# A cross-attention and FFN kernel: transposes and scores of one pair in turn, and the end of attention in parts of one pair

## The chip, the cores and the metric

The kernel runs on one core of a Trainium2 chip. A core has five engines with a queue each: TensorE (PE; its weight loads are shown apart as PEld), VectorE (DVE), ScalarE (ACT), GpSimd (POOL) and SyncE (SP), which mostly issues DMAs. They run side by side and wait for each other on semaphores. TensorE writes to PSUM, which has 8 banks; DVE and ACT empty them. The metric is the device time of one execution in microseconds (us); lower is better.

## The reference

32 batches of 100 rows of 256 features attend to a context of 361 rows each, with 16 heads of 64; after that comes an FFN of 1024 features with quantised weights and activations. All data are float32.

```python
x = x + _L0_xattn_ref(_layernorm(x, axis=-1), ctx_1024, ctx_1024, WQ, WK, WV, WO, mask)
x = x + _L0_ffn_ref(_layernorm(x, axis=-1), W1, b1, W2, b2)

# attention
Qh = jnp.einsum('btd,hdk->bhtk', Q, WQ)
Kh = jnp.einsum('btd,hdk->bhtk', K, WK)
Vh = jnp.einsum('btd,hdv->bhtv', V, WV)
logits = jnp.einsum('bhtk,bhsk->bhts', Qh, Kh) / jnp.sqrt(dk)
logits = logits + mask * -1000000000.0
attn = jax.nn.softmax(logits, axis=-1)
Ah = jnp.einsum('bhts,bhsv->bhtv', attn, Vh)
A = jnp.transpose(Ah, (0, 2, 1, 3)).reshape(Ah.shape[0], Ah.shape[2], -1)
return A @ WO

# FFN: both linear layers on integers, the scale from the whole tensor's minimum and maximum
h = _qlinear(x, W1, b1)
h = jax.nn.gelu(h, approximate=False)
out = _qlinear(h, W2, b2)
```

The scale of the activations is taken over all rows of all batches, so the FFN cannot begin before the attention of the last batch is complete.

## The kernel before

The attention is a list of steps. A step is one batch and some of its 8 pairs of heads: batch 0 is cut into steps of 2, 2 and 4 pairs, batch 31 into 4, 2 and 2, and each of the 30 batches between is one step of all 8 pairs ("whole-batch steps"). TensorE's order is exactly the order in which the program issues its instructions; the other engines' orders are set by a scheduler, which keeps the order of dependent instructions and the extra orders that the program states with `follow(a, b)` (a after b on one engine, without a semaphore).

In step i TensorE runs, in this order:

1. `weights_T(i - 1, pair)` for each pair of the step before (L405, tile pt). The softmax weights p of a head are transposed in three chunks, the lower and the upper half of the rows side by side in two 64-row tiles of the array, each into a bank of its own. One bank is copied to SBUF (tile pT) by DVE (L416), the other by ACT (L418).
2. `scores(i)` (L364, tile sc): two heads of a pair side by side, again in two 64-row tiles, one bank each. DVE adds the mask, writes p and finds the row's minimum m of the negated scores in one instruction (L376); this frees the bank. ACT takes the exponential in place and sums the row (L379). Then DVE takes reciprocals of four heads' sums at a time (L387) and multiplies each head by its own (L391).
3. `attend(i - 1)` (L434, tile av): values times transposed weights, four pairs to a bank, copied to aT by ACT (L441).
4. `v_part` (L276, tile pv): the values of this batch, six banks, copied by DVE (L283).
5. Work on groups of four batches: layer norm and its transposes (ptx L325), queries (pq L337), output projection (py L470) and its transposes back (po L484); for the last group the projection by batch, `project` (po L454).
6. `k_part` (L245, tile pk): the keys of the next step, one bank a pair, copied to kT by ACT (L252).

All these tiles take PSUM banks from one pool of 8, in the order in which they are issued. So a new tile waits until the tile that stands eight before it has been emptied.

`residual(b, y)` adds the projection to x, keeps minimum, maximum and moments, and for all batches but the last leaves `normalize(b)` (L132, on DVE) for later, for it needs a power that GpSimd computes. For the last batch the root is taken on ACT (L504, then the table of Gelu at L507). The main loop runs the waiting `normalize` calls in the next step, after a value copy.

After the loop comes the tail of the last step (batch 31, pairs 6 and 7): `project(B - 1, range(4))`, the transposes of both pairs, projection chunk 4, `attend` for both pairs, and chunks 5 to 7. ACT loads the table with the square root (L385, tile g0) at the end of `scores` of the last step. Then the maximum over all rows sets the quantisation, and the FFN starts.

Of the kernel before, what the change touches and what calls it, by code (L numbers as in the profile page):

```python
# [8 lines left out]
F32 = mybir.dt.float32  # L9
BF16 = mybir.dt.bfloat16  # L10
I16 = mybir.dt.int16
AF = mybir.ActivationFunctionType
ALU = mybir.AluOpType
# [8 lines left out]
BIG = 3.4e38  # L22
# [5 lines left out]
def kernel(  # L28
# [15 lines left out]
    nc = tc.nc  # L44
    P = 128
    B, T, D = x.shape
# [48 lines left out]
    def follow(a, b):  # L95

        tc.add_manual_dep(a.ins, b.ins.name, ORDER)
# [31 lines left out]
    def normalize(b, after):  # L129

        xb = xg[b // G][:, b % G, :]
        i = nc.vector.tensor_scalar(  # L132
            xb, xb, mv2[:, b, 0:1], rstd2[:, b : b + 1], ALU.subtract, ALU.mult
        )
        follow(i, after)
# [13 lines left out]
    with ExitStack() as att:  # L149
# [30 lines left out]
        def bank(name):  # L180
            return psum.tile([P, 512], F32, tag="ps", name=name)
# [165 lines left out]
                    -1.0 / DK**0.5, None, ALU.mult,  # L347
                )

        def scores(i):  # L350


            b, first, n = steps[i]
            g, j = b // G, b % G
            heads = range(2 * first, 2 * (first + n))
            rsum = small.tile([TP, 2 * NHP], F32, tag="rsum", name=f"rsum{i}")
            r = small.tile([TP, 2 * NHP], F32, tag="r", name=f"r{i}")
            for h0 in heads[::4]:
                four = range(h0, h0 + 4)
                pss = {}  # L360
                for h in four:
                    pair, k = divmod(h, 2)
                    pss[h] = bank(f"sc{i}_{h}")
                    nc.tensor.matmul(  # L364
                        pss[h][:TP, :S],
                        qbuf[pair // PAIRS][
                            k * DK : (k + 1) * DK, pair % PAIRS, j, :, :
                        ].rearrange("p k t -> p (k t)")[:, :TP],
                        kT[k * DK : (k + 1) * DK, pair, :],
                        start=True,  # L370
                        stop=True,
                    )
                for h in four:
                    s = pb[:, h, :S]
                    m = small.tile([TP, 1], F32, tag="m", name=f"m{i}_{h}", bufs=8)
                    found = nc.vector.tensor_tensor_reduce(  # L376
                        s, pss[h][:TP, :S], maskt, 1.0, BIG, ALU.add, ALU.min, m
                    )
                    nc.scalar.activation(  # L379
                        s, s, AF.Exp, bias=m, scale=-1.0, accum_out=rsum[:, h : h + 1]  # L380
                    )
            if i == len(steps) - 1:

                g0 = small.tile([T, 1], F32, tag="g0", name="g0")
                nc.scalar.activation(g0, rsum[:T, heads[-1] : heads[-1] + 1], AF.Sqrt)  # L385
            for h0 in heads[::4]:
                last = nc.vector.reciprocal(r[:, h0 : h0 + 4], rsum[:, h0 : h0 + 4])  # L387
                follow(last, found)
                for h in range(h0, h0 + 4):
                    s = pb[:, h, :S]  # L390
                    nc.vector.tensor_scalar(s, s, r[:, h : h + 1], None, ALU.mult)  # L391
            return last

        pTs, aTs = {}, {}

        def weights_T(i, pair):


            h0 = 2 * pair
            pts = [bank(f"pt{i}_{pair}_{k}") for k in range(2)]  # L400
            for h in range(2):
                for c in range(NSC):
                    for k in range(2):
                        ks = slice(k * RH, k * RH + TH)
                        nc.tensor.transpose(  # L405
                            pts[k][:SC, (h * NSC + c) * TH : (h * NSC + c + 1) * TH],
                            pb[ks, h0 + h, c * SC : (c + 1) * SC],
                            ident[ks, ks],
                        )
            pT = pTs[i, pair] = p1.tile(  # L410
                [SC, 2 * NSC, 2, TH], F32, tag=f"pT{pair}", name=f"pT{i}_{pair}"
            )
            for k in range(2):
                src = pts[k][:SC, : 2 * NSC * TH].rearrange("p (c t) -> p c t", t=TH)
                if k == 0:
                    nc.vector.tensor_copy(pT[:, :, k, :], src)  # L416
                else:
                    nc.scalar.copy(pT[:, :, k, :], src)  # L418

        def attend(i):  # L420


            b, first, n = steps[i]
            g, j = b // G, b % G
            if first == 0 and j == 0:
                aTs[g] = p1.tile([P, NHP, G, T], F32, tag="aT", name=f"aT{g}")
            for p0 in range(first, first + n, HP):
                m = min(HP, n)
                av = bank(f"av{i}_{p0}")
                for pair in range(p0, p0 + m):  # L430
                    for c in range(NSC):
                        for k in range(2):
                            h = 2 * (pair % HP) + k
                            nc.tensor.matmul(  # L434
                                av[k * DK : (k + 1) * DK, (pair - p0) * T : (pair - p0 + 1) * T],
                                vs[b, pair // HP][:, c, h * DK : (h + 1) * DK],
                                pTs[i, pair][:, k * NSC + c, :, :].rearrange("p k t -> p (k t)"),
                                start=(c == 0),
                                stop=(c == NSC - 1),
                            )  # L440
                nc.scalar.copy(  # L441
                    aTs[g][:, p0 : p0 + m, j, :],
                    av[:, : m * T].rearrange("p (c t) -> p c t", t=T),
                )

        pos = {}

# [133 lines left out]
        for i, (b, first, n) in enumerate(steps):  # L581
            g, j = b // G, b % G
            begun = [h for h in range(2) if first <= h * HP < first + n]
            ended = [h for h in range(2) if first < (h + 1) * HP <= first + n]
            if i >= 1:
                _, p0, m = steps[i - 1]
                for pair in range(p0, p0 + m):
                    weights_T(i - 1, pair)
            last = scores(i)
            if i >= 1:  # L590
                attend(i - 1)
            if b >= 1:
                for h in begun:
                    for c in range(NSC):
                        done = v_part(b, h, c)
                        if h == begun[0] and c == 0:
                            first_copied = done
                        if c != 2:
                            copied = done
            while later:  # L600
                normalize(later.pop(), copied)
            if b == 0 and first < HP:
                for q in range(1, 2) if first == 0 else range(2, NQ):
                    q_part(0, q)
            for h in ended:
                k = 2 * j + h
                if k < G:
                    stats1((g + 1) * G + k, last)
                if k == 2 * (G - 2) + 1:
                    ln1(g + 1, first_copied)  # L610
                if g >= 1 and 2 <= k < 2 + G:
                    project_back(g - 1, k - 2)
                if k == 2 * (G - 2) + 1:
                    ln1_T(g + 1)
                if j == G - 1:
                    for q in range(2):
                        q_part(g + 1, 2 * h + q)
                if g >= 1 and k == 1:
                    for dc in range(NDC):
                        project_T(g - 1, dc)  # L620
                if h == 1 and b + NCB < B:
                    load_ctx(b + NCB)
            if g == NG - 1 and j >= 1 and 1 in begun:
                project(b - 1, range(NHP))
            if i + 1 < len(steps):
                for pair in range(steps[i + 1][2]):
                    k_part(i + 1, pair)
            if i >= 3:
                for w, p in todo[:2]:
                    quantize_weight(*weights[w], w, p, last)  # L630
                del todo[:2]

        project(B - 1, range(4))
        for pair in range(NHP - PAIRS, NHP):
            weights_T(len(steps) - 1, pair)
        project(B - 1, range(4, 5))
        attend(len(steps) - 1)
        project(B - 1, range(5, 6))
        project(B - 1, range(6, NHP))
        warm(bank("warm1"), 12)  # L640


# [207 lines left out]
```

## Time and profile before

| | us |
|---|---|
| median of 3 runs | 1350.59 |
| lowest and highest | 1350.57, 1351.49 |
| the profiled execution | 1350.39 |
| its span, first to last instruction | 1348.6 |

The busy table counts the time in which an engine has something running; TensorE's instructions overlap each other, so its share says that it is occupied, not that it works at its peak. The granted TensorE clock was 0.993 of full speed. The chain of waits is read from the last instruction back: at each step the profile goes to whatever released the instruction, or to the one before it on its engine. A piece "PE sc L364 x32" is 32 records of TensorE for line 364; a float32 matmul leaves two records, a transpose one. The length of a piece is from the end of the piece before to its own end, so it contains waiting and the cost of a change of stage. Square brackets in the timeline name idle time of the engine before the line, and what ended it. A whole-batch step takes about 33 to 44 us, by the group work in it.

### The profile page before, as it was taken

The numbers are of one execution on the slowest core, as the hardware profiler recorded it, in microseconds if no ns is written. First come the engines' busy times: TensorE is split into PE (matmuls) and PEld (weight loads), VectorE is DVE, ScalarE is ACT, GpSimd is POOL, SyncE is SP. The second block draws the span as 40 slices with busy tenths as digits, with TensorE's granted clock in tenths as the row PEclk, the third lists the DMA queues.
The fourth block names the chain that finished last, engine by engine and source line by source line (L and its number), as shares of the span: only waits on it lengthen the run. The fifth ranks groups of instructions, "written<-read, shape, count | busy, mean of one in ns | idle before, by whom it ended". The sixth has DMA issues, their size and how long they took to land.

```text
span 1348.6 us, 25655 instructions
## 1 busy us (share of the span) xinstructions
PE 1311.7 (97%) x10062; PEld 820.0 (61%) x10064; DVE 835.4 (62%) x2580; ACT 623.8 (46%) x1711; POOL 86.9 (6%) x181
## 2 busy tenths in 40 slices
PE   9999999999999999999999999999999999999747
PEld 4666556666566566666566566665566666666316
DVE  4676446776366565765366664664467653675897
ACT  2555235555355245554255345552355453443845
POOL 1000001200011000110011000110011000110000
PEclk9999999999999999999999999999999999999979
DMA  8010001000000000000000000000000000000202
GB/s 250 22 43 13 11 12 44 25 12 1 12 19 18 12 12 1 19 18 12 11 19 19 12 12 1 18 19 12 12 19 19 13 1 12 10 11 4 82 20 98
DMA packets 24895, 33.02 MB, mean 24 GB/s; under 512 B 1787, under 2 KB 22851, under 8 KB 24774
## 3 DMA queue, kind: packets, MB, share of 16 engines
q1 hardware_dynamic: 21854, 24.91, 6.3%
q0 software_dynamic: 2096, 5.28, 1.3%
q8 instruction: 79, 1.29, 0.4%
q10 hardware_dynamic: 824, 1.19, 0.3%
q14 instruction: 42, 0.34, 0.1%
HBM read 24.82 MB, written 6.55 MB: 23 GB/s over the span
## 4 chain that ended last, share of the span: by engine, by line
PE 93%; issue 5%; DVE 1%; ACT 0%; DMA 0%; POOL 0%; DVEq 0%; POOLq 0%
PE pv L276 25%; PE pk L245 23%; PE sc L364 13%; PE av L434 10%; PE pt L405 7%; PE pq L337 6%; PE py L470 6%; PE pf L798 1%; PE po L454 1%; PE po L484 0%; PE ptx L325 0%; PE pk L259 0%; PE warm L146 0%; DMA out_dram<-ot 0%; ACT p L379 0%
## 5 line engine op out<-in xcount | busy, mean ns | idle before, releaser
L276 PE MATMUL pv<-wvt,c 128*128 128x512 f32 x768 | 338.3, 596 | 0.0
L416 DVE COPY pT<-pt 128x300 f32<-128x300 f32 x256 | 99.9, 461 | 350.8 <-PE pt L405 350.7
L252 ACT COPY kT<-pk 128x361 f32<-128x361 f32 x254 | 117.1, 461 | 427.5 <-PE pk L245 427.5
L245 PE MATMUL pk<-c,wkt 128*128 128x361 f32 x1016 | 314.2, 467 | 0.0
L379 ACT ACTIVATE p<-p,m 114x361 f32<-114x361 f32 x512 | 297.4, 584 | 30.1 <-DVE m L376 30.1
L245 PEld LDWEIGHTS pk<-c,wkt 128*128 128x128 f32 x1016 | 191.9, 190 | 113.2 <-issue 1.0
L276 PEld LDWEIGHTS pv<-wvt,c 128*128 128x128 f32 x768 | 143.3, 190 | 172.1 <-issue 155.7
L376 DVE CUSTOM_DVE_ANT_0 p<-sc,maskt 114x361 f32<-114x361 f32 x512 | 235.4, 531 | 6.4 <-PE sc L364 6.4
L364 PE MATMUL sc<-kT,q 64*114 64x361 f32 x1024 | 176.1, 472 | 0.0
L283 DVE COPY v<-pv 128x512 f32<-128x512 f32 x192 | 127.4, 684 | 66.0 <-PE pv L276 65.7
L391 DVE TENSOR_SCALAR p<-p,r 114x361 f32<-114x361 f32 x512 | 167.4, 401 | 0.6
L434 PEld LDWEIGHTS av<-pT,v 128*64 128x64 f32 x3072 | 132.8, 137 | 18.5 <-DVE m L376 16.6
L434 PE MATMUL av<-pT,v 128*64 128x100 f32 x3072 | 139.8, 250 | 0.0
L364 PEld LDWEIGHTS sc<-kT,q 64*114 64x114 f32 x1024 | 101.0, 176 | 56.5 <-DVE m L376 5.5
L405 PEld LDWEIGHTS pt<-ident,p 50*128 50x128 f32 x3072 | 99.1, 139 | 18.6 <-issue 18.0
L405 PE MATMUL pt<-ident,p 50*128 50x50 f32 x3072 | 103.7, 224 | 0.4 <-DVE p L391 0.4
L418 ACT COPY pT<-pt 128x300 f32<-128x300 f32 x256 | 97.1, 411 | 3.3 <-PE pt L405 0.7
L379 ACT ACTIVATION_READ_ACCUMULATOR p<-p,m 114x1 f32 x512 | 95.8, 187 | 0.0
L337 PE MATMUL pq<-xnT,wqt 128*128 128x400 f32 x256 | 87.9, 500 | 0.2 <-ACT xnT L328 0.2
L125 POOL TENSOR_TENSOR xb<-x,b2a 100x256 f32<-100x256 f32 x31 | 22.9, 738 | 908.2 <-DVE rmax L494 899.2
L470 PE MATMUL py<-aT,wot 128*128 128x400 f32 x224 | 76.4, 499 | 0.0
L337 PEld LDWEIGHTS pq<-xnT,wqt 128*128 128x128 f32 x256 | 48.4, 190 | 38.8 <-issue 3.9
(119 smaller groups left out, 676.5 us busy)
## 6 DMA issues: line engine op xcount, KB each, us to landing
c<-in_ctxT_dram SPq DMA_DIRECT2D x31, 361.0 KB, 3.0
x<-in_x_dram SPq DMA_DIRECT2D x8, 400.0 KB
xb<-xb POOLq DMA_DIRECT2D x31, 100.0 KB, 2.1
x<-xb SPq DMA_DIRECT2D x5, 512.0 KB, 4.9
out_dram<-ot SPq DMA_DIRECT2D x5, 512.0 KB, 2.9
wqt<-in_wq_dram SPq DMA_DIRECT2D x4, 256.0 KB
wot<-in_wo_dram SPq DMA_DIRECT2D x1, 1024.0 KB, 7.8
w<-in_w1T_dram POOLq DMA_DIRECT2D x1, 1024.0 KB, 5.6
```

The source lines that it names most:

```text
L245: nc.tensor.matmul(pk[:, :S], wkt[q][:, dc, col * P : (col + 1) * P], c[:, dc, :S], start=(dc == 0), stop=(dc == NDC - 1),)
L252: nc.scalar.copy(kT[:, first + pair, :], pk[:, :S])
L276: nc.tensor.matmul(pv[:SC, :], c[:, dc, s * SC : (s + 1) * SC], wvt[h][:, dc, :], start=(dc == 0), stop=(dc == NDC - 1),)
L283: return nc.vector.tensor_copy(vs[b, h][:, s, :], pv[:SC, :])
L337: nc.tensor.matmul(pq[:, :GT], wqt[q][:, dc, pair * P : (pair + 1) * P], xnTs[g][:, dc, :], start=(dc == 0), stop=(dc == NDC - 1),)
L364: nc.tensor.matmul(pss[h][:TP, :S], qbuf[pair // PAIRS][k * DK : (k + 1) * DK, pair % PAIRS, j, :, :].rearrange("p k t -> p (k t)")[:, :TP ...
L376: found = nc.vector.tensor_tensor_reduce(s, pss[h][:TP, :S], maskt, 1.0, BIG, ALU.add, ALU.min, m)
L379: nc.scalar.activation(s, s, AF.Exp, bias=m, scale=-1.0, accum_out=rsum[:, h : h + 1])
L391: nc.vector.tensor_scalar(s, s, r[:, h : h + 1], None, ALU.mult)
L405: nc.tensor.transpose(pts[k][:SC, (h * NSC + c) * TH : (h * NSC + c + 1) * TH], pb[ks, h0 + h, c * SC : (c + 1) * SC], ident[ks, ks],)
L434: nc.tensor.matmul(av[k * DK : (k + 1) * DK, (pair - p0) * T : (pair - p0 + 1) * T], vs[b, pair // HP][:, c, h * DK : (h + 1) * DK], pTs[i ...
L470: nc.tensor.matmul(py[:, :GT], wot[:, c, dc * P : (dc + 1) * P], aT[:, c, :, :].rearrange("p j t -> p (j t)"), start=(c == 0), stop=(c == ...
```

## The change

Four things change.

- In whole-batch steps (`turns`) the transposes of pair q of the step before and the scores of pair q of this step are issued in turn: pt, sc, pt, sc and so on, where before all transposes came first. Of the two copies of a pair's transposes DVE makes one for the first pair only; all others are made by ACT. The exponentials of all 16 heads are ordered behind the last of these copies on ACT. Each head has its own m (tags `m0` to `m15`) where eight rotated.
- In the very last step each head's reciprocal is taken by itself.
- The tail of attention goes by one pair: projection chunks 0 and 1, transposes of pair 6, chunks 2 and 3, transposes of pair 7, `attend` of pair 6, chunk 4, `attend` of pair 7, chunks 5 to 7. The normalisation that still waits in the last step is done behind the last copy of pT on DVE.
- The table load for the square root moves from the end of the last `scores` to behind the last aT copy on ACT.

```diff
+        def weights_T(i, pair, on_vector):
...
+            copies = []
             for k in range(2):
                 src = pts[k][:SC, : 2 * NSC * TH].rearrange("p (c t) -> p c t", t=TH)
-                if k == 0:
-                    nc.vector.tensor_copy(pT[:, :, k, :], src)
-                else:
-                    nc.scalar.copy(pT[:, :, k, :], src)
+                copy = nc.vector.tensor_copy if k == 0 and on_vector else nc.scalar.copy
+                copies.append(copy(pT[:, :, k, :], src))
+            return copies
...
         def scores(i):
...
+            turns = n == NHP
...
+            def exponentials(heads):
+                for h in heads:
+                    s = pb[:, h, :S]
+                    done = nc.scalar.activation(
+                        s, s, AF.Exp, bias=ms[h], scale=-1.0, accum_out=rsum[:, h : h + 1]
+                    )
+                    if turns:
+                        follow(done, copied)
...
+            for pairs in ([q] for q in range(first, first + n)) if turns else (
+                range(q, q + PAIRS) for q in range(first, first + n, PAIRS)
+            ):
+                if turns and pairs[0] < before:
+                    copied = weights_T(i - 1, p0 + pairs[0], pairs[0] == 0)[1]
...
+                for h in four:
+                    ms[h] = small.tile([TP, 1], F32, tag=f"m{h}", name=f"m{i}_{h}", bufs=1)
+                    found = nc.vector.tensor_tensor_reduce(
+                        pb[:, h, :S], pss[h][:TP, :S], maskt, 1.0, BIG, ALU.add, ALU.min, ms[h]
+                    )
+                if not turns:
+                    exponentials(four)
+            if turns:
+                exponentials(heads)
+            at_once = 1 if i == len(steps) - 1 else 4
+            for h0 in heads[::at_once]:
+                last = nc.vector.reciprocal(
+                    r[:, h0 : h0 + at_once], rsum[:, h0 : h0 + at_once]
+                )
...
-            while later:
+            while later and i < len(steps) - 1:
                 normalize(later.pop(), copied)
...
-        project(B - 1, range(4))
-        for pair in range(NHP - PAIRS, NHP):
-            weights_T(len(steps) - 1, pair)
-        project(B - 1, range(4, 5))
-        attend(len(steps) - 1)
-        project(B - 1, range(5, 6))
-        project(B - 1, range(6, NHP))
+        i = len(steps) - 1
+        for pair, before in ((NHP - 2, (0, 2)), (NHP - 1, (2, 4))):
+            project(B - 1, range(*before))
+            on_vector = weights_T(i, pair, True)[0]
+        attend(i, (NHP - 2, 1))
+        project(B - 1, range(4, 5))
+        copied = attend(i, (NHP - 1, 1))
+
+        g0 = small.tile([T, 1], F32, tag="g0", name="g0")
+        follow(nc.scalar.activation(g0, epst[:T], AF.Sqrt), copied)
+        for c in range(5, NHP):
+            project(B - 1, range(c, c + 1))
+        normalize(later.pop(), on_vector)
         warm(bank("warm1"), 12)
```

More of the change, by code (lines that the diff above doesn't have):

```diff
@@ L348, in q_part @@
                 )
[L350 to L392, printed above, removed]
         pTs, aTs = {}, {}
-        def weights_T(i, pair):
+        def weights_T(i, pair, on_vector):
             h0 = 2 * pair
@@ L412, in weights_T @@
             )
+            copies = []
             for k in range(2):
                 src = pts[k][:SC, : 2 * NSC * TH].rearrange("p (c t) -> p c t", t=TH)
-                if k == 0:
-                    nc.vector.tensor_copy(pT[:, :, k, :], src)
-                else:
-                    nc.scalar.copy(pT[:, :, k, :], src)
-        def attend(i):
-            b, first, n = steps[i]
+                copy = nc.vector.tensor_copy if k == 0 and on_vector else nc.scalar.copy
+                copies.append(copy(pT[:, :, k, :], src))
@@ new lines, in weights_T, with scores @@
+            return copies
+        def scores(i):
+            b, first, n = steps[i]
+            g, j = b // G, b % G
+            _, p0, before = steps[i - 1] if i else (0, 0, 0)
+            turns = n == NHP
+            heads = range(2 * first, 2 * (first + n))
+            rsum = small.tile([TP, 2 * NHP], F32, tag="rsum", name=f"rsum{i}")
+            r = small.tile([TP, 2 * NHP], F32, tag="r", name=f"r{i}")
+            ms = {}
+            def exponentials(heads):
[7 more added lines that the diff above has]
+            if not turns:
+                for pair in range(p0, p0 + before):
+                    weights_T(i - 1, pair, True)
+            for pairs in ([q] for q in range(first, first + n)) if turns else (
[3 more added lines that the diff above has]
+                    copied = weights_T(i - 1, p0 + pairs[0], pairs[0] == 0)[1]
+                pss = {}
+                four = range(2 * pairs[0], 2 * pairs[-1] + 2)
+                for h in four:
+                    pair, k = divmod(h, 2)
+                    pss[h] = bank(f"sc{i}_{h}")
+                    nc.tensor.matmul(
+                        pss[h][:TP, :S],
+                        qbuf[pair // PAIRS][
+                            k * DK : (k + 1) * DK, pair % PAIRS, j, :, :
+                        ].rearrange("p k t -> p (k t)")[:, :TP],
+                        kT[k * DK : (k + 1) * DK, pair, :],
+                        start=True,
+                        stop=True,
+                    )
+                for h in four:
+                    ms[h] = small.tile([TP, 1], F32, tag=f"m{h}", name=f"m{i}_{h}", bufs=1)
+                    found = nc.vector.tensor_tensor_reduce(
+                        pb[:, h, :S], pss[h][:TP, :S], maskt, 1.0, BIG, ALU.add, ALU.min, ms[h]
+                    )
+                if not turns:
+                    exponentials(four)
[5 more added lines that the diff above has]
+                    r[:, h0 : h0 + at_once], rsum[:, h0 : h0 + at_once]
+                )
+                follow(last, found)
+                for h in range(h0, h0 + at_once):
+                    s = pb[:, h, :S]
+                    nc.vector.tensor_scalar(s, s, r[:, h : h + 1], None, ALU.mult)
+            return last
@@ L424, in attend @@
+        def attend(i, pairs=None):
+            b, first, n = steps[i]
+            if pairs is not None:
+                first, n = pairs
             g, j = b // G, b % G
@@ L440, in attend @@
                             )
-                nc.scalar.copy(
+                copied = nc.scalar.copy(
                     aTs[g][:, p0 : p0 + m, j, :],
@@ L444, in attend @@
                 )
+            return copied
         pos = {}
@@ L584 @@
             ended = [h for h in range(2) if first < (h + 1) * HP <= first + n]
[L585 to L588, printed above, removed]
             last = scores(i)
```

## The prediction

> **What bounds the kernel now.** I read the page's busy table first, then the chain of work that ended last as a whole, then the same chain in order of time for single stages, then the timeline of one step, and at last the chain at the end of attention.
>
> ```profile
> PE 1311.7 (97%) x10062; PEld 820.0 (61%) x10064; DVE 835.4 (62%) x2580; ACT 623.8 (46%) x1711; POOL 86.9 (6%) x181
> ...
> PE 93%; issue 5%; DVE 1%; ACT 0%; DMA 0%; POOL 0%; DVEq 0%; POOLq 0%
> ```
>
> TensorE (PE) is the path: 93% of the chain. The "issue" is one piece of 64.4 us in the FFN, which is not touched. So what counts is the time from one PE stage to the next. The chain in order of time (start, length, what), for the small steps of batch 0 and for one whole-batch step:
>
> ```profile
> 29.83 1.27 PE sc L364 x8
> ...
> 43.59 2.49 PE sc L364 x16
> ...
> 57.16 1.64 PE pt L405 x48
> 58.80 5.33 PE sc L364 x32
> ...
> 385.64 0.44 PE po L484 x4
> ...
> 395.79 3.14 PE pt L405 x96
> 398.93 5.32 PE sc L364 x32
> 404.25 4.27 PE av L434 x96
> 408.52 10.50 PE pv L276 x24
> ```
>
> The reader is to fit a straight line to each kind. Scores (sc) of 2 and 4 pairs take 1.27 and 2.49: 0.61 a pair plus 0.05 for coming from the transposes. Eight pairs at that pace would take 4.93; they take 5.33, so PE loses **0.40 us in each whole-batch step**. Transposes (pt) of 4 and 8 pairs take 1.64 and 3.14: 0.375 a pair plus 0.14 for coming from the key projection. The timeline of another step says whom the scores wait for:
>
> ```profile
> 632.23 0.54 DVE L376 CUSTOM_DVE_ANT_0 p<-sc,maskt 114x361 f32<-114x361 f32 x1 [0.19 <-PE sc L364]
> ...
> 632.68 0.53 DVE L376 CUSTOM_DVE_ANT_0 p<-sc,maskt 114x361 f32<-114x361 f32 x1
> ...
> 635.41 0.08 DVE L376 DVE_READ_ACCUMULATOR2_ANT m<- 114x1 f32 x1
> ...
> 635.55 0.72 PEld L364 LDWEIGHTS sc<-kT,q 64*114 64x114 f32 x4 [0.18 <-DVE m L376]
> ```
>
> VectorE (DVE) empties one head's bank per 0.455 us, PE fills one per 0.305; there are 8 banks, so the last heads wait for DVE (here PE takes the bank 0.06 after the read that frees it). That wait is all that turn-taking can win.
>
> **What the Trainium skill says.** "TensorEngine Tiling", Key Properties: changing the tiling mode, not just the tile, drains TensorE. Transposes and scores both use two 64-row tiles, so alternating should not drain. The trace agrees in the direction it shows: the first score weight load is issued at 631.30 while the transposes still run (to 631.53), whereas coming from the full array to 64-row tiles leaves the weight port idle (0.51 us before pt in the timeline). "TensorE: Matmul & The Clock Gate", Step-by-step: weight loads are pulled ahead of running matmuls, one buffer deep; the same page's LDWEIGHTS section prices a load at columns/1.2 ns, an estimate of 95 ns for 114 columns. Two transposes side by side take 0.0625 (0.375 / 6) and cannot cover that, a score matmul of 0.30 (0.61 / 2 passes) can cover any load here: this is the 0.05 at pt to sc, and why none is due at sc to pt. "ScalarE: Activation LUTs", What ACT_TABLE_LOAD costs: 1283 ns; the page of before has the same 1283.
>
> **The change, part by part.**
>
> *Turns in the 30 whole-batch steps.* PE's instructions are the same, in another order. Batch 1's step has 4 pairs of the previous step to transpose, the other 29 have 8. A turn costs 0.375 + 0.61 + 0.05 = 1.035. The return from scores to the next transposes is not in the trace. Bounds: 0 (the nearest row, a matmul followed by a transpose in one mode: the back-transposes po L484 after pv take 0.44 for 4 and start without a gap) and 0.09 (a drain: 0.14 entry of pt less the 0.05 of a plain weight-bound start). I take 0, for the mode is the same.
> - 8-pair step: 0.14 + 8 x 1.035 = 8.42, against 3.14 + 5.33 = 8.47: -0.05. Times 29: **-1.45**.
> - Batch 1: 0.14 + 4 x 1.035 + 4 x 0.61 = 6.72, against 1.64 + 5.33 = 6.97: **-0.25**.
>
> So the 0.40 that PE waited goes, and 7 more entries of 0.05 (0.35) come in its place.
>
> *Are the banks free in time?* A turn takes four of the 8 banks, so turn q reuses those of turn q-2, 2.07 earlier. Scores: DVE starts 0.86 after the first score matmul (631.37 to 632.23), the second head's maximum lands 0.99 later (0.455 + 0.53), PE sees it 0.06 later: 1.91, and its load must lead by 0.06: about **0.1 spare**, the tightest place. DVE's own pace, 0.91 a turn, is under 1.035. Transposes: 15 of 16 copies go to ScalarE (ACT), two a turn at 0.38 (2.29 for 6): done 1.4 after the turn's start, due at 2.0. DVE's one copy (pair 0, 0.39) ends before the first scores are out. So PE should not wait.
>
> *What the later exponentials do.* All 16 stand behind the last pT copy on ACT: they begin about 8.7 into the step (7.3 for the last turn's start, 0.6 to its first copy, two copies), where they began 4.5 in (632.80 against 628.32). At 0.58 each they end at 18.0 instead of 13.7; the two aT copies behind them end at 18.9. On DVE the reciprocals wait for them, and by the order of the built program the first value copy (v) stands behind the third reciprocal, at 15.8; its matmuls end at 14.5. The first bank of that stage is wanted again when pv ends, at 8.42 + 4.27 + 10.50 = 23.2: over 4 us of cover for aT, over 2 for the v copies. Every fourth step normalises the next four batches behind the fourth reciprocal; they end at about 23.1, wanted at about 24. If that cover went, each us of lateness would cost at most 8 us in all, once in each of the 7 groups. I take 0.
>
> *End of attention.* The chain of before:
>
> ```profile
> 1239.59 0.58 POOL rstd L511
> ...
> 1240.19 0.41 DVE x L132
> 1240.61 0.76 DVE pT L416 x2
> 1241.36 0.44 DVE p L376
> 1241.84 2.44 ACT p L379 x8
> ...
> 1245.07 1.25 PE pt L405 x24
> 1246.32 0.61 PE po L454 x2
> 1246.92 1.18 PE av L434 x24
> 1248.11 1.55 PE po L454 x6
> 1249.68 0.42 DVE x L494
> ```
>
> The last normalisation waits for GpSimd (POOL) and holds up both pT copies; after, it stands behind the last pT copies, so DVE's mask operations start when scores arrive (1240.14 + 0.86 = 1241.0, not 1241.28): -0.28. The reciprocals of heads 1 to 3 are issued before the first division, so the third head's exponential (1243.70 - 0.28 = 1243.42) and a reciprocal (0.18) gate it: first division at 1243.6 instead of 1244.52, PE's first transpose at 1244.15 instead of 1245.07. From there PE does more, for two projections now stand between the pairs: pt of one pair 0.51, po x4 0.94, pt 0.51, av of one pair 0.66, po x2 0.61, av 0.66, po x6 1.5, together 5.39, and 0.14 of waiting for the second division: 1249.7, against 1249.68. What the earlier divisions give, the entries and the projections moved behind them take: **0**, bounds -0.5 and +0.5. The table load (1.28 + 0.2) moves from before the pT copies to behind the last aT copy, about 1248.5 to 1250.0; the square root is due at 1251.0. No cost; were aT over 1 us later, the excess would show. No moved part issues a DMA, and SP's queue stays as it is; behind the moved normalisation DVE has only the last residual, which comes over 2 us later.
>
> *Sum.* -1.45 - 0.25 + 0 = -1.7. The profiled execution took 1350.39 (span 1348.6 and 1.8 around it), 0.2 under the median of 1350.59; so the forecast is 1348.7 on its scale, **1348.9** as a median.
>
> **The rivals.**
> - *Every return drains* (slower). 29 x 7 + 3 = 206 returns from scores to transposes at 0.09: +18.5, 1367. Decides from 0.022 a return (4.4 us). For it: that direction is nowhere in the trace. Against: one mode, and pv to po shows none. Chance 0.12.
> - *PE is paced by DVE in the turns* (slower). The 0.1 spare is used up when ACT's PSUM reads or a late semaphore stretch the loop of two turns; 0.1 over, 0.05 a turn, is 236 x 0.05 = 12: 1361. For it: the spare is small. Against: DVE's pace is 12% quicker than the turn. Chance 0.13.
> - *The 0.05 entry vanishes* (faster), because the score weights are loaded under the transposes: another 29 x 7 x 0.05 = 10, 1339. For it: in the small steps 0.05 is only an intercept of two lines. Against: the load is longer than a transpose. Chance 0.20, partly hidden included.
> - *The forecast*: 0.55.
>
> **How the numbers follow.** What can be told from no change is 0.2%, 2.7 us: 1347.9 to 1353.3. The forecast's own spread (the entry is read to 0.005, times 236; the end to 0.5) is 1346 to 1351.5; of its 0.55, 0.38 lie within the bound, 0.16 below, 0.01 above. Faster 0.16 + 0.20 = 0.36, within 0.38, slower 0.01 + 0.25 = 0.26. The range reaches 1340 to 1362.
>
> **What would show it.** Right: turns of about 1.035 (PE pt and sc alternating, 8.4 from the first pt to the first av), no PEld idle "<-DVE m" inside them, first exponential near 8.7. Wrong: turns of 1.10 or more with idle weight port before pt (drain) or before sc (DVE); turns of 0.99 (entry hidden); v copies that hold PE after pv; a residual (L494's successor) that starts other than 1249 to 1250 less the gain before it.

## The result and the profile after

| | before | after |
|---|---|---|
| median, us | 1350.59 (1350.16 to 1351.95, 7 runs) | 1346.10 (1345.25 to 1349.12, 7 runs) |
| ratio after / before | | 0.9966, 95% interval 0.9956 to 0.9976 |
| forecast, range | | 1348.9, 1340 to 1362 |
| 29 whole-batch steps: first pt to first av | 8.455 to 8.471 | 8.307 to 8.311 |
| batch 1: first pt to first av | 6.967 | 6.659 |
| first pt of the last step to the last residual | 10.33 | 10.34 |

The change is faster by 4.5 us, outside what can be told from no change; the forecast was 1.7 faster. The profiled execution of after took 1349.12 because it started late: PE's second value matmul waited 2.97 for GpSimd's zero-fill of the context buffers (the page has it as "3.0 <-POOL c L171"), and its first scores stand 3.8 later than in the profile of before (25.85 against 22.04). The fill itself is short; GpSimd came to it late, at 13.02 instead of 10.57, and the trace names no cause. The six other runs took 1345.25 to 1346.29. So lengths of steps are compared here, not positions.

The busy table and the shares of the chain, in the page of after:

```profile
PE 1308.6 (97%) x10064; PEld 809.2 (60%) x10064; DVE 784.7 (58%) x2377; ACT 693.2 (51%) x1918; POOL 86.7 (6%) x181
...
PE 93%; issue 6%; DVE 1%; ACT 0%; POOL 0%; POOLq 0%; DVEq 0%
```

PE is still the path. DVE is busy about 50 us less and ACT 69 more, since 206 of the pT copies went from DVE to ACT. The same stretch of a whole-batch step as in the prediction, in the chain in order of time:

```profile
398.07 0.51 PE pt L362 x12
398.57 0.66 PE sc L412 x4
399.24 0.36 PE pt L362 x12
...
405.71 0.66 PE sc L412 x4
406.38 4.27 PE av L457 x96
```

A turn is 0.66 + 0.36 = 1.02, not 1.035. In none of the 29 steps does PE or its weight port wait for DVE or ACT between the first pt and the first av. From the first pt to the first av a step gains 0.15, from there to the next step's first pt nothing (35.22 in both kernels for the longest kind of step). 29 x 0.152 + 0.308 = **4.72**, which covers the whole difference of the medians (4.5).

The end of attention, same view:

```profile
1243.15 0.62 PE pt L362 x12
1243.77 1.04 PE po L478 x4
1244.80 0.51 PE pt L362 x12
...
1247.25 1.48 PE po L478 x6
...
1248.76 0.42 DVE x L518
```

The first pt comes 4.73 after the first pt of the last step (1238.42), where it came 5.72 after it in the kernel before: 1.0 earlier. From there to the residual it takes 5.61 instead of 4.61. The two cancel to 0.01.

### The profile page after: what moved, and what is told of

It is laid out like the page before. It is cut to its first block, busy times and chain, and to the rows that moved or that the text cites. A ratio compares the mean times of both kernels' runs of the same rounds, so it can differ in the third digit from the quotient of the medians.

```text
span 1347.3 us, 25422 instructions
## 1 busy us (share of the span) xinstructions
PE 1308.6 (97%) x10064; PEld 809.2 (60%) x10064; DVE 784.7 (58%) x2377; ACT 693.2 (51%) x1918; POOL 86.7 (6%) x181
## 3 DMA queue, kind: packets, MB, share of 16 engines
q8 instruction: 79, 1.29, 0.4%
## 4 chain that ended last, share of the span: by engine, by line
PE 93%; issue 6%; DVE 1%; ACT 0%; POOL 0%; POOLq 0%; DVEq 0%
PE pv L276 25%; PE pk L245 23%; PE sc L412 13%; PE av L457 10%; PE pt L362 7%; PE pq L337 6%; PE py L494 6%; PE pf L824 2%; PE po L478 1%; PE po L508 0%; PE ptx L325 0%; DVE ot L831 0%; ACT p L393 0%; DVE ih L705 0%; DVE hq L710 0%
## 5 line engine op out<-in xcount | busy, mean ns | idle before, releaser
L423 DVE CUSTOM_DVE_ANT_0 p<-sc,maskt 114x361 f32<-114x361 f32 x512 | 252.3, 533 | 11.8 <-PE sc L412 6.9
L374 DVE COPY pT<-pt 128x300 f32<-128x300 f32 x50 | 22.3, 469 | 351.5 <-PE pt L362 351.5
L412 PE MATMUL sc<-kT,q 64*114 64x361 f32 x1024 | 208.8, 490 | 0.0
L374 ACT COPY pT<-pt 128x300 f32<-128x300 f32 x462 | 169.0, 414 | 73.8 <-PE pt L362 71.2
L362 PEld LDWEIGHTS pt<-ident,p 50*128 50x128 f32 x3072 | 131.9, 139 | 77.4 <-issue 51.1
L438 DVE TENSOR_SCALAR p<-p,r 114x361 f32<-114x361 f32 x512 | 173.6, 404 | 2.6
L362 PE MATMUL pt<-ident,p 50*128 50x50 f32 x3072 | 133.9, 221 | 0.3 <-DVE p L438 0.3
L393 ACT ACTIVATION_READ_ACCUMULATOR p<-p,m 114x1 f32 x512 | 101.9, 199 | 0.0
L412 PEld LDWEIGHTS sc<-kT,q 64*114 64x114 f32 x1024 | 77.1, 184 | 4.3 <-issue 0.6
L432 DVE RECIPROCAL r<-rsum 114x4 f32<-114x4 f32 (+1 forms) x131 | 22.9, 175 | 90.7 <-ACT p L393 90.7
```

Source lines behind the costliest of these rows:

```text
L362: nc.tensor.transpose(pts[k][:SC, (h * NSC + c) * TH : (h * NSC + c + 1) * TH], pb[ks, h0 + h, c * SC : (c + 1) * SC], ident[ks, ks],)
L374: copies.append(copy(pT[:, :, k, :], src))
L393: done = nc.scalar.activation(s, s, AF.Exp, bias=ms[h], scale=-1.0, accum_out=rsum[:, h : h + 1])
L412: nc.tensor.matmul(pss[h][:TP, :S], qbuf[pair // PAIRS][k * DK : (k + 1) * DK, pair % PAIRS, j, :, :].rearrange("p k t -> p (k t)")[:, :TP ...
L423: found = nc.vector.tensor_tensor_reduce(pb[:, h, :S], pss[h][:TP, :S], maskt, 1.0, BIG, ALU.add, ALU.min, ms[h])
```

## The experiments

Two questions were open: whether all of the gain sits in the turns, and why a turn is 0.015 shorter than the sum of its parts in the prediction. PE runs each float32 score matmul in two passes, so a head leaves two records. Starts of PE's records (lower half of the array) around one turn of after, worked out from the trace, in us, with the step from the record before:

```
sc, second pass  630.462
pt 1             630.765   +0.303
pt 2             630.814   +0.049
pt 3             630.874   +0.060
pt 4             630.937   +0.063
pt 5             630.999   +0.062
pt 6             631.060   +0.061
sc, first pass   631.123   +0.063
sc, second pass  631.482   +0.359
```

The loads of the same stretch, from the timeline of the weight port (PEld):

```profile
630.46 0.14 PEld L362 LDWEIGHTS pt<-ident,p 50*128 50x128 f32 x2
630.77 0.39 PEld L362 LDWEIGHTS pt<-ident,p 50*128 50x128 f32 x10 [0.16 <-issue]
631.06 0.30 PEld L412 LDWEIGHTS sc<-kT,q 64*114 64x114 f32 x4
```

The load for pt 1 starts with the score's second pass (630.46) and is over at 630.60; the port then idles for 0.16 until pt 1 starts. So pt 1 finds its weights in place.

Over the 203 returns from scores to transposes of the 29 steps, the step from the score's second pass to pt 1 is 0.303 to 0.304, that from pt 1 to pt 2 0.048 to 0.049; all other steps between transposes have a median of 0.062, as in the kernel before. Such a step is called the pitch below. My theory after the result (Theory A of the runs from the seventh to the ninth): a turn is two score passes of 0.303, and between them PE waits for its weight port only. The load for pt 1 runs under the score's second pass, so five transpose loads are paid, not six; the score's own load is paid in full. Rivals: transposes in turn are all a little quicker; the 0.056 at the score (0.359 - 0.303) is a fixed cost of the change from transposes to matmuls; part of the gain comes from the end.

**1. The turns alone.**

```diff
-            at_once = 1 if i == len(steps) - 1 else 4
...
+            at_once = 4
...
-            while later and i < len(steps) - 1:
+            while later:
...
-        i = len(steps) - 1
-        for pair, before in ((NHP - 2, (0, 2)), (NHP - 1, (2, 4))):
...
+        project(B - 1, range(4))
+        for pair in range(NHP - PAIRS, NHP):
+            weights_T(len(steps) - 1, pair, True)
...
```

> The turns of the whole-batch steps alone, with the end of attention of the kernel before (all of its parts: projections 0 to 3 first, both pairs' transposes together, reciprocals by four, the normalisation ahead of the copies, the table load where it was). My theory: the whole gain sits in the turns. First transposes to first av 8.31 in 29 steps against 8.46, and 6.66 against 6.97 in batch 1: 29 x -0.152 - 0.31 = -4.7 us against the kernel before. Rival: the end in parts is worth the 1 us by which its first transposes came earlier, so this kernel shows -3.7 or less.

Measured 1345.79 against 1350.96, ratio 0.9962 (0.9949 to 0.9974). Steps of 8.307 to 8.311 and 6.661. The whole gain is there; the rival, that the end is worth 1 us of it, falls.

**2. The end alone.**

```diff
-            turns = n == NHP
+            turns = False
```

> The steps of the kernel before (all transposes, then all scores), with the new end of attention and the moved table load. My theory: 0 (-0.3 to +0.3) against the kernel before: the first transposes of the last pairs come 1 us earlier and PE then has 1 us more to do before the last residual. Rival: -1.0, if the later part were hidden.

Measured 1350.62 against 1350.96, ratio 0.9998 (0.9990 to 1.0007). The residual starts 10.33 after the step's first pt, as before. The end in parts is worth nothing.

**3. Turns of two pairs.**

```diff
-            for pairs in ([q] for q in range(first, first + n)) if turns else (
-                range(q, q + PAIRS) for q in range(first, first + n, PAIRS)
-            ):
+            for pairs in (range(q, q + PAIRS) for q in range(first, first + n, PAIRS)):
                 if turns and pairs[0] < before:
-                    copied = weights_T(i - 1, p0 + pairs[0], pairs[0] == 0)[1]
+                    for q in pairs:
+                        copied = weights_T(i - 1, p0 + q, q == 0)[1]
```

> Turns of two pairs in place of one: pt, pt, sc, sc. Theory A, that the banks decide: a turn uses all 8 banks, DVE starts 0.86 after the first score, takes 0.455 a head, and so the fourth bank is free about 2.8 after it, while PE would load for it at 2.5 in the next turn: a wait of about 0.3 in each of three turns of a step, less 0.15 for four entries fewer: about +0.7 a step, +20 us against the kernel after the change (about 1366). Theory B, that the entry from transposes to scores decides: four entries of 0.055 fewer and four covered loads of 0.014 fewer, -0.16 a step, -4.5 us (about 1341.5).

Measured 1350.37, 4.3 above after; a step takes 8.46. Four turns without a wait would be 8.17 (0.79 to the first score, three turns of 2.006, and the 1.365 that run 12 shows from the first score of such a turn to the first av), so the banks cost 0.29 a step. This is Theory A of this run in kind, but a third of its size: it asked for 0.3 in each of three turns. The chain shows why:

```profile
631.53 1.31 PE sc L411 x8
632.85 0.74 PE pt L362 x17
633.59 0.06 PE sc L411
633.65 0.12 PE pt L362 x2
```

In the second turn the fourth head's load stands at 632.18, where the third head's stands at 632.03, for DVE reads its bank until 632.12. Only the upper half of the array waits. The lower half goes on: in the next turn its scores start at 633.43, and the last three transposes of the upper half, which were issued before them, start between 633.43 and 633.55. The lag of 0.19 is kept, not paid again: the turns have 2.01, 2.06 and 2.01 from first score to first score. It is paid once, at the end of the step, where av takes the whole array: by then the upper half is 0.24 behind, and av starts 0.39 after the start of the upper half's last pass, as it does in after.

**4. Six projection chunks first.** An attempt at the end of attention, on top of after.

```diff
-        for pair, before in ((NHP - 2, (0, 2)), (NHP - 1, (2, 4))):
-            project(B - 1, range(*before))
+        project(B - 1, range(6))
+        for pair in (NHP - 2, NHP - 1):
             on_vector = weights_T(i, pair, True)[0]
         attend(i, (NHP - 2, 1))
-        project(B - 1, range(4, 5))
         copied = attend(i, (NHP - 1, 1))
...
-        for c in range(5, NHP):
+        for c in range(6, NHP):
```

> The kernel after the change with another order at the end: projection chunks 0 to 5 first, then the transposes of both pairs, attend of both, chunks 6 and 7. Chunks 4 and 5 then stand where PE waits for the first division, and three chunks fewer stand behind the second pair's transposes. The second pair's transposes still wait for their own division. Expected: last residual 0.4 to 0.8 earlier relative to the first transposes of the last batch, the time -5.0 to -5.4 against the kernel before. Rival: the copies of pT and aT, which the moved chunks covered, come late instead and it gains nothing.

Measured 1344.96 (ratio to before 0.9960, 0.9946 to 0.9974). The residual starts 9.65 after the step's first pt instead of 10.34: 0.7 gained. The transposes of pair 6 come later than in after:

```profile
1238.14 2.76 PE po L478 x12
```

The six chunks keep PE until 1240.84, 6.10 after the step's first pt; in after the transposes start 4.73 after it, 1.4 earlier. PE is not waiting in this stretch: the twelve passes start 0.216 apart without a gap. The aT that chunk 4 needs is copied by 1239.60 and the load for it starts at 1239.67, as early as the passes ahead of it allow.

**5. Exponentials not ordered behind the copies.**

```diff
-                    if turns:
-                        follow(done, copied)
```

> The kernel after the change without the order that puts a step's exponentials behind the last copy of pT on ACT; the program then has two exponentials after each turn's copies. My theory: ACT then has 0.72 + 2 x 0.58 = 1.9 a turn against PE's 1.02, the banks of the transposes come free late, and each step loses 2.5 to 4 us: +70 to +115 us against the kernel after. Rival: the order is not needed, since ACT catches up behind the scores: within 2 us of the kernel after.

Measured 1446.08 (one execution, as in the next two runs): +100. A step takes 11.73. In its chain ACT is the path:

```profile
679.54 0.61 ACT pT L374 x2
680.15 0.63 ACT p L393 x3
...
681.31 0.61 ACT pT L374 x2
```

A turn is 1.77 there, two copies and two exponentials. So the late exponentials, which cost nothing, are what the turns live on.

**6. DVE makes one copy of every pair.**

```diff
-                    copied = weights_T(i - 1, p0 + pairs[0], pairs[0] == 0)[1]
+                    copied = weights_T(i - 1, p0 + pairs[0], True)[1]
```

> The kernel after the change with DVE making one of the two pT copies of every pair, as before the change, where it made that of the first pair alone. My theory: DVE then has 1.02 + 0.39 = 1.4 a turn against PE's 1.02, with about 0.1 spare in the banks: 6 turns of a step lose 0.39 less the spare, +2.0 to +2.3 a step, +58 to +67 us against the kernel after. Rival: the spare of the banks is larger than I read it and half or less of that shows.

Measured 1382.00: +36, a step of 9.54. The kind is right and the size is not. DVE's cycle is two masks of 0.455 and a copy of 0.38, 1.29 and not 1.4 (the expectation added the copy to 1.02, which holds DVE's idle time already). The loss also starts late: turns 1 to 4 start 1.02 apart. From turn 5 on the weight port waits, in the timeline of PEld:

```profile
648.74 0.17 PEld L412 LDWEIGHTS sc<-kT,q 64*114 64x114 f32 x1 [0.17 <-DVE m L423]
...
650.03 0.17 PEld L412 LDWEIGHTS sc<-kT,q 64*114 64x114 f32 x1 [0.18 <-DVE m L423]
```

This is the picture of the rival "paced by DVE": 1.29 apart, each turn ended by a maximum. Nothing of it is in the trace of after.

**7. Transposes made twice** (all pairs but the first of a step; the second time into the same place).

```diff
-            for h in range(2):
+            for h in (0, 1) if on_vector else (0, 1, 0, 1):
                 for c in range(NSC):
```

> The transposes of each pair but the first of a step are made twice, into the same place (same result). Theory A: a transpose costs its weight load, 0.0625 for two side by side, and only the first two after a score matmul find theirs done (0.049): 12 more transposes add 0.375 to each of 206 turns: a turn is 1.395, +77.3 us against the kernel after. Theory B: all transposes in a turn are cheaper, 0.358 / 6 each: a turn of 1.378, +73.7 us.

Measured 1423.85: +77.75. Twelve more transposes, six on each half, cost 0.376 a turn ((10.94 - 8.31) / 7). That is Theory A: a transpose costs its 0.0625 in the turns too, and only the one after the score is cheap (0.048 to 0.049, again).

**8. Scores of 70 rows.**

```diff
+            QP = 70
...
-                        pss[h][:TP, :S],
+                        pss[h][:QP, :S],
...
-                        ].rearrange("p k t -> p (k t)")[:, :TP],
+                        ].rearrange("p k t -> p (k t)")[:, :QP],
```

> Scores, exponentials and divisions of the first 70 of the 114 rows only; the rows from 70 on keep zeros as weights, so 44 of 100 rows of each batch get no attention. The weight load of a score matmul has 70 columns in place of 114; its moving side, and DVE's and ACT's lengths, stay. Theory A: the entry of 0.055 from transposes to scores is the part of the load (0.115) that two transposes (0.06) do not cover: the load then takes 0.07, the entry falls to about 0.01, a turn is 0.975: -10.6 us against the kernel after. Theory B: the entry is a fixed cost of the change from transposes to matmuls: a turn stays at 1.02 and the time within 1 us.

This kernel leaves out the attention of 44 of the 100 rows of each batch and is for the measurement only. The 29 steps shrink to 8.01 to 8.02; from the first whole-batch step to the last the gain is 8.65. The score's second pass follows its first by 0.323 instead of 0.359, so a turn is 0.984. The extra 0.056 at the score is no fixed cost: it goes with the columns, 0.036 for 44 of them, 0.82 ns each. That is the price in the Trainium skill ("TensorE: Matmul & The Clock Gate", LDWEIGHTS: columns / 1.2 ns, 0.83 ns a column). The expectation asked for 0.045 a turn. The time as a whole, 1342.97, shows only 3.1 of it, because filling the unused rows with zeros takes GpSimd 4.92 at the start and stands on the chain.

**9. Chunks of 121.**

```diff
-    SC = P
+    SC = 121
```

> The kernel after the change with the 361 context rows cut into three chunks of 121 instead of 128, so that a transpose's weight load has 121 columns in place of 128. From the score loads (114 columns 0.115, 70 columns 0.079, two loads each) a column costs 0.41 ns in one load. Theory A, the pitch of the transposes is their weight load: 0.0625 becomes 0.0596, 5 of 6 in a turn and 6 of 6 elsewhere: about -0.015 a pair, -0.12 a step, -3.6 us against the kernel after (about 1342.5), and turns of 1.006. Theory B, the pitch is a fixed cost of issuing an instruction: turns stay at 1.020 and the time within 0.5 us.

Measured 1405.68, ratio to before 1.0403 (1.0389 to 1.0417): 63 us above the time of Theory A and 60 above that of Theory B. The edit also changes the value projection (its loads have 121 columns) and attend (121 rows), but the loss is in the transposes: from the first pt to the first av a step is 1.78 longer, which makes 52 of the 60 us in the 29 steps. A pair's transposes in a turn take 0.57 instead of 0.36, in the chain:

```profile
654.62 0.57 PE pt L362 x12
655.20 0.66 PE sc L412 x4
```

The first step after a score is 0.048 as before, all others are 0.103 to 0.106 (0.062 in after). This fits Theory A, that the pitch is the weight load: where the load is covered, nothing has changed. But the load of 121 columns is longer than that of 128. The groups of weight loads show it; the number after the busy time is the mean of one in ns. First after:

```profile
L245 PEld LDWEIGHTS pk<-c,wkt 128*128 128x128 f32 x1016 | 191.9, 190 | 113.2 <-issue 1.0
L457 PEld LDWEIGHTS av<-pT,v 128*64 128x64 f32 x3072 | 132.8, 137 | 18.5 <-ACT pT L374 15.0 <-DVE m L423 1.6 <-issue 1.6
L362 PEld LDWEIGHTS pt<-ident,p 50*128 50x128 f32 x3072 | 131.9, 139 | 77.4 <-issue 51.1 <-DVE q L344 0.5 <-DVE pT L374 0.4
...
L508 PEld LDWEIGHTS po<-ident,yT 128*100 128x100 f32 x56 | 6.6, 128 | 7.6 <-issue 6.1 <-DVE v L283 1.2 <-DVE am L560 0.2
```

and the kernel with chunks of 121:

```profile
L362 PEld LDWEIGHTS pt<-ident,p 50*121 50x121 f32 x3072 | 198.4, 182 | 69.0 <-issue 17.9 <-DVE q L344 0.5 <-DVE pT L374 0.4
```

The matmuls lie on one line: 64 columns 137, 128 columns 190, 0.83 ns a column. 121 columns on that line are 184, and the transposes of 121 have 182. Transposes of 128 (139) and of 100 columns (128) lie far below it; the two points are 0.4 ns a column apart. So a transpose's load can be much quicker than a matmul's, and with 121 columns it is not. With chunks of 121 the places where the chunks start in p move too (484 bytes apart, not 512). That does not explain it: the first chunk of a row of p starts where it did, and its load takes 177 in the 29 steps (135 in after); chunks 16 and 32 start at multiples of 64 bytes from the beginning of the row and take 183.

**10. Two chunks behind the first transposes**, the end once more.

```diff
-        for pair, before in ((NHP - 2, (0, 2)), (NHP - 1, (2, 4))):
+        for pair, before in ((NHP - 2, (0, 4)), (NHP - 1, (4, 6))):
...
-        project(B - 1, range(4, 5))
...
-        for c in range(5, NHP):
+        for c in range(6, NHP):
```

> The kernel after the change with the end reordered once more: chunks 0 to 3, transposes of pair 6, chunks 4 and 5, transposes of pair 7, attend of both, chunks 6 and 7. Chunks 4 and 5 wait for aT of pairs 4 and 5, which is ready by then, so the first transposes start as early as after the change (4.73 behind the start of the step's first transposes; with six chunks first it was 6.10), and two chunks fewer stand behind the second attend. Expected: last residual 1.0 to 1.4 earlier than after the change, about 9.1 behind the step's first transposes (10.34 after, 9.65 with six chunks first). Rival: the second division still gates, and pT's copies then the aT copy hold the last chunk, so that it gains no more than six chunks first (0.7).

Measured 1345.20 (ratio to before 0.9953, 0.9940 to 0.9965). The residual starts 9.82 after: half a microsecond gained, less than with six chunks first. The time of the rival came out, but not for its reason. Four chunks take 1.90 (1238.03 to 1239.93 in its chain), so PE itself is late with the first transposes (5.24 after the step's first pt, where 4.73 was expected), and from there PE works almost without a gap.

**11. Chunks of 121 with that end.**

> Chunks of 121 and the reordered end together. If each keeps its own gain: their sum, about -4.8 us against the kernel after (-9.4 against the kernel before, ratio 0.993). If the shorter turns use up the spare of the banks (0.12, of which two turns of 1.006 take 0.03), less of it shows.

Measured 1404.85, where about 1341 was expected: the loss of the ninth run, and a residual 0.47 earlier than in it (10.85 after the step's first pt against 11.32). It tells nothing new.

**12. A last turn of two, six chunks first.** What the runs had given, put together.

```diff
-            for pairs in ([q] for q in range(first, first + n)) if turns else (
+            for pairs in ([[q] for q in range(6)] + [[6, 7]]) if turns else [
...
-                    copied = weights_T(i - 1, p0 + pairs[0], pairs[0] == 0)[1]
+                    for q in pairs:
+                        copied = weights_T(i - 1, p0 + q, q == 0)[1]
```

> Six turns of one pair and a last turn of two (pt, pt, sc, sc), with six chunks first at the end. Theory A, loads and banks as the other runs gave them: the last turn saves one entry of 0.055 and loses one covered load of 0.014, and no bank is late (the transposes of pair 7 take the banks of pair 4's scores, free 2.33 after that turn began and wanted at 2.34; the scores of pair 7 those of pair 5's, free at 3.35 and wanted at 3.4, both counted from the start of turn 4): first transposes to first av 8.27 in 29 steps against 8.31, -1.2 us; with the -0.7 of six chunks first -1.9 against the kernel after (about 1344.2). Theory B: a bank is late as in the turns of two pairs throughout (0.29 a step over four turns), and the step is 8.31 to 8.4: 0 to +2 us, less 0.7.

Measured 1343.84 against 1350.65, ratio 0.9951 (0.9938 to 0.9965), the lowest median of the kernels that leave nothing out. Steps of 8.270 to 8.276, as Theory A has it; the end keeps its 9.65. The scores of the sixth turn and the last turn, in its chain:

```profile
630.86 0.66 PE sc L413 x4
631.52 0.73 PE pt L362 x24
632.25 1.27 PE sc L413 x8
```

## Why the prediction came out as it did

- **The direction and the mechanism** were right: the wait for DVE between scores goes, and entries (the extra time of a score that follows transposes) come in its place. The size was not: 4.5 us came for 1.7. The step that failed is one term of the sum, the **0.375 in "A turn costs 0.375 + 0.61 + 0.05 = 1.035"**. It is the slope of transposes among themselves and holds six weight loads. The prediction says that a score matmul "can cover any load here" and draws from it only that the return costs nothing; that it also takes one load out of the six it does not count. Measured: 0.36, of which the transpose after the score has 0.048 instead of 0.0625 in every one of 203 returns. 29 x 7 + 3 = 206 returns times 0.0145 make the 3.0 us by which 4.72 exceeds the predicted 1.70. Shown by the records, by transposes made twice (+0.376 for twelve with no score ahead) and by chunks of 121 (0.048 after a score, 0.103 to 0.106 elsewhere). The time alone would not have told: 1346.1 is at the edge of the forecast's own spread (1346 to 1351.5), and an entry that is partly hidden would have given it too. Only the starts of the records tell the two apart. It was luck, too, that a faster kernel could be told at all: the forecast of 1.7 lies within what cannot be told from no change (2.7), and the gain went beyond that by the term that the sum did not have.
- **The entry of 0.05** stands at 0.056 (0.359 - 0.303). Its rival "vanishes" falls. The 70 columns show that it is the score's weight load.
- **The return at 0** holds: 0.303 in every return, the time of a score pass where no load is waited for. "Every return drains" falls.
- **The spare of 0.1** was well read: the second head's maximum is read until 631.96 and the load that needs its bank stands at 632.08, 0.12 later. "Paced by DVE" falls for this kernel. But my use of such a spare elsewhere was too strict: with DVE's copies four turns pass before it shows, and in turns of two pairs a wait of one half is paid once.
- **What hides the late exponentials**: they start 8.4 into the step and end at 17.7 (predicted 8.7 and 18.0), the first v copy at 15.6 (15.8), aT at 18.6 (18.9). The four layer norms of the next group end at 22.0 and are wanted at 23.3 (23.1 and 24). A step takes the same from av to the next pt as before. Their cost of 0 is shown; so is, at +100 us, what it costs when they go between the copies.
- **The end at 0** holds in the trace (10.34 against 10.33) and in a run of its own (0.9998). Its parts: first pt 1.0 earlier (0.92 predicted), then 5.61 to the residual (5.53).
- **The table load** ends at 1248.84 and the tile after it at 1249.05; the square root starts at 1250.09. 1.0 of cover was left.

Left open: what a chunk of 122 or 124 columns would do (not tried; the 100-column transposes, 128 ns a load, suggest that a full 128 is not what makes the quick load, but they use the full height of the array and not its halves), and how much the tail would gain with the first transposes at 4.7 and six chunks out of its way (in both orders tried the chunks ahead of them keep PE busy until later).

## What to carry to other kernels

- When two kinds of PE work are interleaved, don't price a turn by the slopes of the kinds alone: ask for each weight load what runs above it. Here a transpose's load under a score pass of 0.303 cost nothing, and the first transpose behind it took 0.048 instead of 0.062.
- A reorder on one engine needs its consumers put in order too: here the same turns are 4.5 us faster than before or 95 slower, by where ACT takes the exponentials.
- An end that starts 1 us earlier is worth nothing if the work moved into it takes that 1 us; measure a tail from a fixed point ahead of it to its last instruction.

## What the runs showed of the hardware

- The load of a float32 transpose does not simply grow with its columns: 128 columns have a pitch of 0.062, 121 columns one of 0.106. Float32 matmuls don't have the quick load (128 columns: 190 ns a record against 139). The Trainium skill ("TensorE: Matmul & The Clock Gate", Weight-path perf modes) gives a fast weight load to 128 weights of a type other than float32; the transposes here are float32 and load quickly at 128 and at 100 columns. Whether it is that mode was not shown.
- The two 64-row halves of the array run apart: in turns of two pairs one waits for a bank while the other goes on, 0.19 ahead, into the scores that were issued behind transposes which the late half has still to start. The lag is paid once, where a stage takes the whole array.
- A late start moved the scores of the profiled execution of after by 3.8 us against that of before, almost the size of what was to be measured: GpSimd reached its zero-fill 2.45 later, and PE waited for it. The comparison by steps was needed to see the rest.
